# Two attention layers on one core: x in sixteen equal parts almost to the end of the pair tensor, and TensorE's order at the end of the prologue written out with the group norm's sums amid it

## The chip, the cores and the metric

The kernel runs on one core of a Trainium2 chip. The metric is device time in microseconds (us), the median of several runs of the whole kernel. The engines are named as the profile names them: PE (TensorE's matrix multiplications; its weight loads are listed as PEld), DVE (VectorE), ACT (ScalarE), POOL (GpSimd) and SP (SyncE, which here only issues transfers). Each engine works through its own instructions in order and waits where an operand or a buffer isn't ready.

## The reference

The input x has the shape (1, 128, 256, 256): 128 rows of 256 tokens with 256 channels. Two layers are applied, each as x plus an attention over the group norm of x:

```python
def _gn(v, G=32, eps=1e-5):          # over rows, tokens and the channels of a group
    g = v.reshape(B_, H_, W_, G, C_ // G)
    m = jnp.mean(g, axis=(1, 2, 4), keepdims=True)
    s = jnp.var(g, axis=(1, 2, 4), keepdims=True)
    return ((g - m) / jnp.sqrt(s + eps)).reshape(v.shape)

# layer 0: 8 heads of 32 channels, gated, with a bias from the pair tensor
bias = jnp.einsum('nijz,zh->nhij', pair_repr, bias_proj)[:, None]
sim = jax.nn.softmax(einsum(q, k) * scale, axis=-1) + bias
attend = jnp.einsum('nshqk,nskhc->nsqhc', sim, v) * gate

# layer 1: 4 heads of 64 channels, each query sees the keys within 16 positions
x = x + _L0_conv_ref(_gn(x), ...)
x = x + _L1_conv_ref(_gn(x), ..., 16)
```

The group norm needs the mean and the variance of each of 32 groups over the whole of x (32 MiB) before the first row of layer 0 can be normalised. The pair tensor (256 x 256 x 128, 32 MiB as well) is reduced to a bias per head, query and key, which stays on the chip for the whole of layer 0.

## The kernel before

The kernel has three stages: a **prologue** (to about 195 us of the span), **layer 0** and **layer 1**, which handle the 128 rows one after the other. Only the prologue is touched.

The prologue reads pair and x, each once. Its loop (line 479) runs over NM = 32 pieces of the pair tensor, 1 MiB each:

- `load_pair(m)` (422) issues the load of piece m on SP's queue into a ring of five buffers (`pr`).
- `turn_pair(m)` (430): sixteen PE transposes into four PSUM banks (`pz`, line 436), each bank copied out by ACT (`prt`, 438).
- `weigh_pair(m - 1)` (441): four matmuls with the bias weights (`pb`, 445, sixteen records in the profile), copied out by ACT (`bs`, 449).
- `place_bias(m - 2)` (452): four transposes (`pbt`, 461), copied out by ACT (`bq`, 462). After every eighth piece eight more transposes (`pbq`, 470) and two copies (471) write a part of `bias_sb`.

Beside the pieces the loop loads x in NX parts (`x_load`, 320; ring of three `xs` buffers of 2 MiB), also on SP's queue, and DVE takes their sums: `x_stats` (327) issues 32 `bn_stats` for a part, one for each group. Before the change PARTS (317) is fifteen parts of 2 MiB and two of 1 MiB, NX = 17. With AHEAD = 27 the last part is issued at m = 26, behind the load of pair piece 26. At part n the statistics of part n - 2 are issued; at the last part, those of the last two.

The group norm's sums are taken in two steps. `group_most` (209) joins the sums of all parts but the last LATE = 3 (`joined`, 184: seven DVE instructions on 896 elements). After the loop `group_columns` (221) joins this with the last three parts (the `_all` tiles, 224 elements), averages over the partitions with a PE product (`ps_m`, 228), adds the spread between partitions on DVE (230 to 232), brings means and variances into columns with four more PE products (`ps_c`, 245), and takes the root on ACT (254, with a table load in front) and the reciprocal on DVE (`rstd`, 256). Then `weigh_pair(31)`, `place_bias(30)` and `place_bias(31)` follow.

The first two rows of x in the layout of layer 0 come by `load(0)` and `load(1)` (348), four transfers each (`xg`); in before `load(0)` is issued right behind the last part of x, and `load(1)` by the first `normal` of layer 0. Layer 0 begins with `normal(0)` and `normal(1)` (686: DVE transposes `xt` at 523 and the normalisation `xn` at 699), `sum_rows(0)` (705: POOL, `ts`, 552 to 555) and `stretch` (818), whose first products are the PE instructions `pq` of line 577.

What sets the order: in the prologue a scheduler orders each engine's instructions by its own estimate of their times, and the program's order is what it starts from. In layers 0 and 1 the order on PE, ACT and DVE is written out (`tc.manual_schedule`). PSUM has five banks in one ring for all products called `proj` or `sim` in the prologue. The prologue's buffers are given back at its end, and tiles of layer 0 take their place.

Of the kernel before, what the change touches and what calls it, by code (L numbers as in the profile page):

```python
# [39 lines left out]
def conv_preact_kernel(  # L40
# [35 lines left out]
    def proj_bank(name):  # L76
        return bank("proj", name)
# [76 lines left out]
    class Quarters:  # L154
# [9 lines left out]
        def sum(self):  # L164
            s1, s2, s3, s4, n11 = (self.sums[:, n, :] for n in range(len(NS)))
            w00, w10, w01, w11 = (self.quarter(kt, m) for m in range(2) for kt in range(2))
            nc.gpsimd.tensor_tensor(s1, w01, w11, ALU.add)
            nc.gpsimd.tensor_tensor(s2, s1, w00, ALU.subtract)
            nc.gpsimd.tensor_tensor(s3, w00, w01, ALU.subtract)
            nc.gpsimd.tensor_tensor(s4, w10, s2, ALU.subtract)  # L170
            nc.gpsimd.tensor_scalar(n11, w11, -1.0, None, op0=ALU.mult)
# [14 lines left out]
    def joined(pool, mean, squares, sizes, name):  # L186

        n, total = len(sizes), sum(sizes)
        share = pool.tile([P, n], F32, name=f"share_{name}")
        for m, size in enumerate(sizes):  # L190
            nc.gpsimd.memset(share[:, m : m + 1], size / total)
        share = share.unsqueeze(1).to_broadcast([P, G, n])
        dev = pool.tile([P, G, n], F32, name=f"dev_{name}")
        nc.vector.tensor_tensor(dev, mean, share, ALU.mult)
        means = pool.tile([P, G], F32, name=f"means_{name}")
        nc.vector.tensor_reduce(means, dev, axis=AX.X, op=ALU.add)
        nc.vector.tensor_tensor(dev, mean, means.unsqueeze(2).to_broadcast([P, G, n]), ALU.subtract)
        nc.vector.tensor_tensor(dev, dev, dev, ALU.mult)
        nc.vector.tensor_tensor(dev, dev, share, ALU.mult)
        nc.vector.scalar_tensor_tensor(dev, squares, 1.0 / total, dev, op0=ALU.mult, op1=ALU.add)  # L200
        inner = pool.tile([P, G], F32, name=f"inner_{name}")
        nc.vector.tensor_reduce(inner, dev, axis=AX.X, op=ALU.add)
        return means, inner
# [14 lines left out]
        nc.vector.tensor_scalar(last[:, :, 0, 1], inner, sum(halves[0:n]), None, op0=ALU.mult)  # L218
        return last

    def group_columns(pool, last, stats, sizes, which):

        tri, halves = group_shares(stats, sizes)
        n = len(halves) - 2 * LATE
        nc.vector.tensor_copy(last[:, :, 1:, :], tri[:, :, n:, 1:3])
        means, v = joined(pool, last[:, :, :, 0], last[:, :, :, 1], [sum(halves[0:n])] + halves[n:], "all")
        ps_m = proj_bank(f"ps_m{which}")
        nc.tensor.matmul(ps_m[:, 0, 0:G], lhsT=avg, rhs=means, start=True, stop=True)
        d = pool.tile([P, G], F32, name=f"d{which}")
        nc.vector.tensor_tensor(d, means, ps_m[:, 0, 0:G], ALU.subtract)  # L230
        nc.vector.tensor_tensor(d, d, d, ALU.mult)
        nc.vector.tensor_tensor(v, v, d, ALU.add)

        wide = pool.tile([P, 2, 2, A, B // CG, CG], F32, name=f"wide{which}")
        for k, what in enumerate((means, v)):
            by_half = what.rearrange("p (a h u) -> p h a u", a=A, h=2)
            for half in range(2):
                nc.vector.tensor_copy(
                    wide[:, k, half], by_half[:, half].unsqueeze(3).to_broadcast([P, A, B // CG, CG])
                )  # L240
        flat = wide.rearrange("p k h a u c -> p k (h a u c)")
        ps_c = proj_bank(f"ps_c{which}")
        for k in range(2):
            for half in range(2):
                nc.tensor.matmul(
                    ps_c[:, 0, 2 * k + half : 2 * k + half + 1],
                    lhsT=flat[:, k, half * P : (half + 1) * P],
                    rhs=avg[:, 0:1],
                    start=True, stop=True,
                )  # L250
        mean = const.tile([P, 2], F32, name=f"mean{which}")
        nc.vector.tensor_copy(mean, ps_c[:, 0, 0:2])
        std = pool.tile([P, 2], F32, name=f"std{which}")
        nc.scalar.activation(std, ps_c[:, 0, 2:4], AF.Sqrt, bias=eps)
        rstd = const.tile([P, 2], F32, name=f"rstd{which}")
        nc.vector.reciprocal(rstd, std)
        return mean, rstd

    class Most:

# [53 lines left out]
    NT = S * R // P  # L314
    TCH = min(16, NT)

    PARTS = [TCH] * (NT // TCH - 1) + [TCH // 2, TCH // 2]
    NX = len(PARTS)

    def x_load(pool, src, n, name):  # L320
# [27 lines left out]
    def load(g):  # L348
        if g < len(GROUPS) and g not in xgs:
            n, s0 = GROUPS[g], sum(GROUPS[:g])  # L350
            xg = big.tile([P, XG * (R // B), C // A], F32, tag="xg", name=f"xg{g}")
            for a in range(A):
                nc.sync.dma_start(out=xg[strip(a), 0 : n * (R // B)], in_=in_strips(x[0], s0, n, a))
            xgs[g] = xg


    with ExitStack() as early:
        pr_pool = early.enter_context(tc.tile_pool(name="pr", bufs=5))
        xs_pool = early.enter_context(tc.tile_pool(name="xs", bufs=3))
        st_pool = early.enter_context(tc.tile_pool(name="st", bufs=1))  # L360
# [61 lines left out]
        def load_pair(n):  # L422

            qt, jc = divmod(n, R // JC)
            pr = pr_pool.tile([P, JC, Z], F32, tag="pr", name=f"pr{n}")
            nc.sync.dma_start(out=pr, in_=pair[0, qt * P : (qt + 1) * P, jc * JC : (jc + 1) * JC, :])
            prs[n] = pr
# [13 lines left out]
        def weigh_pair(m):  # L441

            pb = ps_av.tile([P, 512], F32, tag=("z", "bv")[m % 2], name=f"pb{m}")
            for g, prt in enumerate(prts.pop(m)):
                nc.tensor.matmul(
                    pb[B * g : B * (g + 1), :], lhsT=bias_w_sb, rhs=prt, start=True, stop=True
                )
            bs = prt_pool.tile([P, 4, P], F32, tag="bs", name=f"bs{m}", bufs=2)
            nc.scalar.copy(bs.rearrange("p i j -> p (i j)"), pb)
            pbs[m] = bs  # L450

        def place_bias(m):

            qt, key = divmod(16 * m, R)
            kt, key = divmod(key, P)
            if key == 0:
                by_query[0] = prt_pool.tile([P, H0, P], F32, tag="bq", name=f"bq{m}", bufs=1)
            bq, bs = by_query[0], pbs.pop(m)
            pt = ps_av.tile([P, 4, 4, B], F32, tag="av", name=f"pbt{m}")
            for i in range(4):  # L460
                nc.tensor.transpose(pt[:, i].rearrange("p g h -> p (g h)"), bs[:, i, :], ident)
            nc.scalar.copy(
                bq[:, :, key : key + 16].rearrange("p h (g i) -> p h g i", i=4),
                pt[:, :, :, 0:H0].rearrange("p i g h -> p h g i"),
            )
            if key == P - 16:
                for h4 in range(0, H0, 4):
                    pq = sim_bank(f"pbq{m}_{h4}").rearrange("p a b -> p (a b)")
                    for h in range(4):
                        nc.tensor.transpose(pq[:, h * P : (h + 1) * P], bq[:, h4 + h, :], ident)  # L470
                    nc.scalar.copy(
                        bias_sb[:, kt, h4 : h4 + 4, qt * P : (qt + 1) * P], pq.rearrange("p (h q) -> p h q", q=P)
                    )
# [1 line left out]
        NM = NPR * (JC // 16)  # L475
        sizes = [k * CG for k in PARTS]

        xss, AHEAD = {}, NM - NM // 6
        for m in range(NM):
            if m % (JC // 16) == 0:  # L480
                load_pair(m // (JC // 16))
            for n in range(m * NX // AHEAD, min((m + 1) * NX // AHEAD, NX)):
                if n == NX - LATE + 2:
                    last = group_most(st_pool, stats, sizes)
                if n >= 2:
                    x_stats(stats, xss[n - 2], n - 2)
                xss[n] = x_load(xs_pool, x[0], n, "0_")
                if n == NX - 1:
                    load(0)
                    for late in (NX - 2, NX - 1):  # L490
                        x_stats(stats, xss[late], late)
            turn_pair(m)
            if m >= 1:
                weigh_pair(m - 1)
            if m >= 2:
                place_bias(m - 2)
            if m == NM // 4:
                load_weights()
                for weights in quarters.values():
                    weights.sum()  # L500
            if m == NM * 3 // 4:
                turn_weights()
        mean0, rstd0 = group_columns(st_pool, last, stats, sizes, 0)
        weigh_pair(NM - 1)
        place_bias(NM - 2)
        place_bias(NM - 1)


    def normalized(pool, xt, mean, rstd, name):
# [846 lines left out]
```

## Time and profile before

| | us |
|---|---|
| median of three runs (lowest, highest) | 3221.67 (3220.45, 3223.09) |
| the profiled execution's own time | 3221.78 |
| its span | 3220.1 |
| PE busy, share of the span | 3135.4 (97%) |
| DVE busy | 2657.6 (83%) |
| last part of x issued, and its statistics done | 150.0 and 172.9 |
| last pair piece issued | 168.3 |
| `rstd` of layer 0 done | 191.9 |
| first product of layer 0 that needs `ts` | 195.6 |

The profile is one execution. Times in it count from the start of the span; "idle before" is the time in which an engine stood still in front of an instruction, with what ended the wait. The table of windows gives each engine's busy time in a stretch, the granted clock of PE (1.00 is full) and the rate of all transfers.

### The profile page before, as it was taken

Reading aid. Unit: us, or ns where it says so; the run is one execution under the profiler, and the core shown is the slowest. Engines: PE = TensorE matmul, PEld = TensorE weight load, DVE = VectorE, ACT = ScalarE, POOL = GpSimd, SP = SyncE. Lnnn points to the kernel's source line nnn. Section 1 sums busy time; section 2 is a strip of 40 time slices with the busy share of each in tenths; the row PEclk is TensorE's granted clock in tenths of the full one; section 3 lists DMA queues with packets and bytes.
Section 4 is the critical chain, followed back from the end, with each engine's and each line's share of the span. In section 5 each row is a group of like instructions: output and inputs, shape, how many; then the busy total and the mean of one; then the engine's idle time right before and its main releaser. Section 6 shows DMA issues by size and latency. Waiting matters only on the chain.

```text
span 3220.1 us, 86853 instructions
## 1 busy us (share of the span) xinstructions
PE 3135.4 (97%) x36965; PEld 2456.0 (76%) x36965; DVE 2657.6 (83%) x3539; ACT 2015.2 (63%) x4316; POOL 1693.7 (53%) x1662
## 2 busy tenths in 40 slices
PE   6799999999999999999999999999999999999997
PEld 4467777777777777777777777678888888888886
DVE  4759999999999999999999999847677777777776
ACT  4566666666666666666666666465666666666664
POOL 3034444444444444444444444287777777777775
PEclk9999999999999999999999999999999999999999
DMA  9931111111111111111111111012222222222222
GB/s 379 421 99 54 48 40 41 34 36 39 40 35 37 38 41 34 38 37 41 34 39 36 41 34 33 22 28 55 67 55 66 67 65 56 67 67 58 64 67 48
DMA packets 346332, 209.38 MB, mean 65 GB/s; under 512 B 273609, under 2 KB 339153, under 8 KB 339665
## 3 DMA queue, kind: packets, MB, share of 16 engines
q1 hardware_dynamic: 345040, 201.37, 21.8%
q8 instruction: 293, 4.80, 0.6%
q0 software_dynamic: 752, 2.36, 0.2%
q14 instruction: 103, 0.84, 0.1%
q10 hardware_dynamic: 144, 0.00, 0.0%
HBM read 136.59 MB, written 67.11 MB: 63 GB/s over the span
## 4 chain that ended last, share of the span: by engine, by line
PE 92%; DMA 4%; DVE 3%; issue 0%; POOL 0%; ACT 0%; SPq 0%; DVEq 0%; ACTq 0%; POOLq 0%
PE sim L717 8%; PE p1v L962 7%; PE 1po L648 7%; PE po L648 7%; PE av L749 7%; PE bv L749 7%; PE pv L581 6%; PE pq L577 6%; PE pk L577 5%; PE p1q L577 5%; PE pg L577 5%; PE p1k L577 5%; PE zs L763 4%; DMA xs<-in_x_dram 4%; PE 1sim L983 3%; PE 1avz L1015 2%
## 5 line engine op out<-in xcount | busy, mean ns | idle before, releaser
L730 ACT ACTIVATE ex<-sim 128x512 f32<-128x512 f32 x1024 | 547.6, 605 | 429.8 <-PE sim L717 429.8
L1043 DVE RECIPROCAL 1rz<-1z 128x512 f32<-128x512 f32 x128 | 427.9, 3343 | 314.8 <-ACT 1z L1037 314.8
L739 DVE TENSOR_TENSOR both<-ex 128x512 f32<-128x512 f32 x512 | 483.8, 983 | 75.4 <-ACT ex L730 75.4
L779 DVE RECIPROCAL d<-d 128x512 f32<-128x512 f32 x128 | 429.1, 3353 | 4.4
L604 POOL TENSOR_TENSOR v<-v,twovg 128x256 f32<-128x256 f32 x64 | 75.5, 1180 | 548.1 <-ACT twovg L622 548.1
L717 PE MATMUL sim<-q,k 32*128 32x256 f32 x4096 | 295.7, 401 | 1.1 <-ACT ex L730 1.1
L648 PE MATMUL po<-at,out_sb 128*128 128x256 f32 x1024 | 285.0, 382 | 4.3 <-DVE at L797 4.3
L648 PE MATMUL 1po<-1at,w_out_t 128*128 128x256 f32 x1024 | 270.2, 388 | 1.1 <-issue 1.0
L717 PEld LDWEIGHTS sim<-q,k 32*128 32x128 f32 x4096 | 186.6, 184 | 102.5 <-issue 94.6
L749 PE MATMUL bv<-bias_sb,v 128*32 128x256 f32 x4096 | 244.5, 379 | 0.7 <-DVE t L794 0.7
L993 POOL TENSOR_TENSOR 1p<-1ex,seen 128x768 f32<-128x768 f32 x128 | 232.5, 1817 | 23.7 <-ACT 1ex L991 23.7
L749 PE MATMUL av<-ex,v 128*32 128x256 f32 x4096 | 244.5, 379 | 0.0
L962 PEld LDWEIGHTS p1v<-w_in_t,1xn 128*64 128x64 f32 x4096 | 222.3, 137 | 21.5 <-issue 21.5
L962 PE MATMUL p1v<-w_in_t,1xn 128*64 128x128 f32 x4096 | 237.7, 274 | 0.3 <-PE warm L886 0.3
L648 PEld LDWEIGHTS 1po<-1at,w_out_t 128*128 128x128 f32 x1024 | 190.3, 191 | 50.2 <-ACT 1z L1037 22.3
L648 PEld LDWEIGHTS po<-at,out_sb 128*128 128x128 f32 x1024 | 185.7, 191 | 25.7 <-issue 4.3
L604 POOL TENSOR_TENSOR q<-q,twoqk 128x256 f32<-128x256 f32 x64 | 48.1, 752 | 297.3 <-ACT twoqk L622 297.3
L749 PEld LDWEIGHTS bv<-bias_sb,v 128*32 128x32 f32 x4096 | 133.2, 110 | 88.7 <-issue 1.1
L749 PEld LDWEIGHTS av<-ex,v 128*32 128x32 f32 x4096 | 133.2, 110 | 87.8 <-issue 0.3
L605 POOL TENSOR_TENSOR 1q<-1q,mid1q 128x512 f32<-128x512 f32 x64 | 81.7, 1277 | 188.6 <-ACT 1q L601 188.6
L699 DVE TENSOR_SCALAR xn<-xt,mean,rstd 128x256 f32<-128x256 f32 x256 | 179.7, 741 | 0.0
L1000 POOL TENSOR_TENSOR 1zp<-1p 128x512 f32<-128x512 f32 x128 | 162.7, 1271 | 10.0
(263 smaller groups left out, 7674.3 us busy)
## 6 DMA issues: line engine op xcount, KB each, us to landing
pr<-in_L_conv_pair_repr_dram SPq DMA_DIRECT2D x32, 1024.0 KB, 23.3
x<-o SPq DMA_DIRECT2D x64, 512.0 KB, 3.0
yg<-x SPq DMA_DIRECT2D x64, 512.0 KB, 4.1
out_dram<-1o SPq DMA_DIRECT2D x256, 128.0 KB, 4.1
xg<-in_x_dram SPq DMA_DIRECT2D x252, 128.0 KB, 3.2
xs<-in_x_dram SPq DMA_DIRECT2D x15, 2048.0 KB, 21.8
xs<-in_x_dram SPq DMA_DIRECT2D x2, 1024.0 KB, 17.6
qkv_sb<-in_L_conv_qkv_proj_dram POOLq DMA_DIRECT2D x4, 192.0 KB, 12.8
```

Of the source, the lines that this page charges most:

```text
L577: nc.tensor.matmul(out, lhsT=weights, rhs=moving, start=first, **flags)
L581: nc.tensor.matmul(out[:, cols], lhsT=moving[:, cols], rhs=weights, start=first and t2 == 0, **flags)
L648: nc.tensor.matmul(ps[:, m, :], lhsT=w[:, kt, m * P : (m + 1) * P], rhs=at[:, kt, :], start=(kt == 0), stop=(kt == 1),)
L699: nc.vector.tensor_scalar(xns[i][:, 2 * r + half, :], xt[:, half, :], mean0[:, half : half + 1], rstd0[:, half : half + 1], op0=ALU.subtra ...
L717: nc.tensor.matmul(sims[j][:, kt, :], lhsT=k[p0 : p0 + D0, 2 * r + half, kt * P : (kt + 1) * P], rhs=q[p0 : p0 + D0, 2 * r + half, :], sta ...
L730: nc.scalar.activation(ex[:, j], sims[j], AF.Exp, scale=1.0 / math.sqrt(D0))
L739: nc.vector.tensor_tensor(both[:, j : j + 2], ex[:, j : j + 2, 0, :], ex[:, j : j + 2, 1, :], ALU.add)
L749: nc.tensor.matmul(to[D0 * j : D0 * (j + 1), half, :], lhsT=v[:, 2 * r + half, c0 : c0 + D0], rhs=weights(4 * half + j, kt), start=(kt == ...
L779: nc.vector.reciprocal(d, d)
L962: nc.tensor.matmul(ps[KB * half : KB * (half + 1), b, :], lhsT=xns[i][:, 2 * r + kt, KB * b : KB * (b + 1)], rhs=w_in_t[:, kt, 2 * C + P * ...
L993: nc.gpsimd.tensor_tensor(p.rearrange("p j (r c) -> p (j r) c", c=WROW)[:, :, 0 : 2 * WSTEP] .rearrange("p r (t c) -> p r t c", c=WSTEP)[: ...
L1043: nc.vector.reciprocal(st[s]["rz"], st[s]["z"])
```

## The change

x comes in sixteen equal parts (`PARTS`), and AHEAD becomes NM - 2 = 30, so that part n is issued at the piece m for which (m + 1) * 16 // 30 first exceeds n: two pieces of pair for a part, in two places one. The last part, number 15, is issued at m = 29; behind it on SP's queue are pair pieces 30 and 31. `group_most` is issued at part 15 too and joins parts 0 to 12.

`load(0)` and `load(1)` move to m = 31, behind the load of pair piece 31.

From m = 29 to the end of the prologue PE's order is the program's. `group_columns` becomes a generator of three pieces: the DVE join of all parts; `ps_m` and the DVE work that follows; `ps_c`, the root and `rstd`. `weigh_pair(31)` comes between the first and the second piece, `place_bias(30)` between the second and the third, and `place_bias(31)` last. On PE this gives, behind the transposes of piece 31: `pb` of 30, `pbt` of 29, `pb` of 31, `ps_m`, `pbt` of 30, `ps_c`, `pbt` of 31, `pbq`.

```diff
@@ -218,12 +218,13 @@
         nc.vector.tensor_scalar(last[:, :, 0, 1], inner, sum(halves[0:n]), None, op0=ALU.mult)
         return last
 
-    def group_columns(pool, last, stats, sizes, which):
+    def group_columns(pool, last, stats, sizes, which, got):
 
         tri, halves = group_shares(stats, sizes)
         n = len(halves) - 2 * LATE
         nc.vector.tensor_copy(last[:, :, 1:, :], tri[:, :, n:, 1:3])
         means, v = joined(pool, last[:, :, :, 0], last[:, :, :, 1], [sum(halves[0:n])] + halves[n:], "all")
+        yield
         ps_m = proj_bank(f"ps_m{which}")
         nc.tensor.matmul(ps_m[:, 0, 0:G], lhsT=avg, rhs=means, start=True, stop=True)
         d = pool.tile([P, G], F32, name=f"d{which}")
@@ -239,6 +240,7 @@
                     wide[:, k, half], by_half[:, half].unsqueeze(3).to_broadcast([P, A, B // CG, CG])
                 )
         flat = wide.rearrange("p k h a u c -> p k (h a u c)")
+        yield
         ps_c = proj_bank(f"ps_c{which}")
         for k in range(2):
             for half in range(2):
@@ -254,7 +256,7 @@
         nc.scalar.activation(std, ps_c[:, 0, 2:4], AF.Sqrt, bias=eps)
         rstd = const.tile([P, 2], F32, name=f"rstd{which}")
         nc.vector.reciprocal(rstd, std)
-        return mean, rstd
+        got += [mean, rstd]
 
     class Most:
 
@@ -314,7 +316,7 @@
     NT = S * R // P
     TCH = min(16, NT)
 
-    PARTS = [TCH] * (NT // TCH - 1) + [TCH // 2, TCH // 2]
+    PARTS = [TCH] * (NT // TCH)
     NX = len(PARTS)
 
     def x_load(pool, src, n, name):
@@ -475,10 +477,16 @@
         NM = NPR * (JC // 16)
         sizes = [k * CG for k in PARTS]
 
-        xss, AHEAD = {}, NM - NM // 6
+        xss, AHEAD = {}, NM - 2
+        tail = early.enter_context(ExitStack())
         for m in range(NM):
+            if m == NM - 3:
+                tail.enter_context(tc.manual_schedule(engines={mybir.EngineType.PE}))
             if m % (JC // 16) == 0:
                 load_pair(m // (JC // 16))
+            if m == NM - 1:
+                load(0)
+                load(1)
             for n in range(m * NX // AHEAD, min((m + 1) * NX // AHEAD, NX)):
                 if n == NX - LATE + 2:
                     last = group_most(st_pool, stats, sizes)
@@ -486,7 +494,6 @@
                     x_stats(stats, xss[n - 2], n - 2)
                 xss[n] = x_load(xs_pool, x[0], n, "0_")
                 if n == NX - 1:
-                    load(0)
                     for late in (NX - 2, NX - 1):
                         x_stats(stats, xss[late], late)
             turn_pair(m)
@@ -500,10 +507,17 @@
                     weights.sum()
             if m == NM * 3 // 4:
                 turn_weights()
-        mean0, rstd0 = group_columns(st_pool, last, stats, sizes, 0)
+        got = []
+        columns = group_columns(st_pool, last, stats, sizes, 0, got)
+        next(columns)
         weigh_pair(NM - 1)
+        next(columns)
         place_bias(NM - 2)
+        for _ in columns:
+            pass
+        mean0, rstd0 = got
         place_bias(NM - 1)
+        tail.close()
 
 
     def normalized(pool, xt, mean, rstd, name):
```

## The prediction

> **What bounds the kernel now.** I first read engine totals and slices on the page, then the prologue by windows, then the single instructions of DVE and PE at its end.
>
> ```profile
> PE 3135.4 (97%) x36965; PEld 2456.0 (76%) x36965; DVE 2657.6 (83%) x3539; ACT 2015.2 (63%) x4316; POOL 1693.7 (53%) x1662
> ...
> GB/s 379 421 99 54 48 40 41 34 36 39 40 35 37 38 41 34 38 37 41 34 39 36 41 34 33 22 28 55 67 55 66 67 65 56 67 67 58 64 67 48
> ```
>
> PE bounds the whole; only the first two slices (80.5 us each) and part of the third run at the memory's rate. Nothing of layers 0 and 1 is edited, so the change can only move the moment at which layer 0 starts: about 195 us of 3220.
>
> ```profile
> 150.00:158.00 8.00, 4.19 (x24) 3.84 (x24) 7.82 (x12) 2.59 (x6) 0.00 (x0) 0.79 1.01 420
> 158.00:168.00 10.00, 9.43 (x75) 7.07 (x73) 10.00 (x60) 7.66 (x23) 0.00 (x0) 1.00 1.06 329
> 168.00:178.00 10.00, 9.63 (x74) 5.78 (x72) 8.05 (x49) 7.51 (x17) 0.00 (x0) 1.00 0.96 348
> 178.00:188.00 10.00, 10.00 (x85) 6.99 (x83) 0.00 (x0) 8.40 (x18) 1.50 (x4) 1.00 0.03 10
> 188.00:196.00 8.00, 5.29 (x37) 3.29 (x36) 4.94 (x15) 3.79 (x8) 4.08 (x11) 1.00 0.24 45
> ```
>
> Columns after the stretch: PE, PEld, DVE, ACT, POOL busy, PE's clock, DMA share, GB/s. Transfers fill the time to about 175. From 158 to 188 PE is full: the loads of x are over after pair piece 26, pieces 27 to 31 then arrive every 2.5 us, and PE needs 3.33 us for one (the `pz` starts 177.66, 181.04, 184.37). So it works off a backlog; the last piece, issued at 168.3, has landed 13.5 us later, at 181.8, and is turned from 184.37. DVE meanwhile is idle.
>
> ```profile
> 172.91 0.36 DVE L225 COPY last<-stats 128x384 f32<-128x384 f32 x1
> ...
> 173.79 0.39 DVE L196 TENSOR_REDUCE means_all<-dev_all 128x32 f32<-128x224 f32 x1
> ...
> 175.94 0.39 DVE L202 TENSOR_REDUCE inner_all<-dev_all 128x32 f32<-128x224 f32 x1
> 188.04 0.19 DVE L230 TENSOR_TENSOR d<-means_all,ps_m 128x32 f32<-128x32 f32 x1 [11.71 <-PE ps_m L228]
> ...
> 191.75 0.17 DVE L256 RECIPROCAL rstd<-std 128x2 f32<-128x2 f32 x1 [1.05 <-ACT std L254]
> ```
>
> The sums of x stand ready at 174.2 and 176.3, and DVE waits 11.7 us for `ps_m`, which is behind the pair's work on PE. The end of PE's part:
>
> ```profile
> 187.69 0.31 PE L228 MATMUL ps_m<-means_all,avg 128*128 128x32 f32 x2
> ...
> 188.35 1.07 PE L445 MATMUL pb<-prt,bias_w_sb 128*32 128x512 f32 x8
> ...
> 195.64 0.70 PE L577 MATMUL pq<-ts,sums_q 128*128 128x256 f32 x2 [1.18 <-POOL ts L552]
> ```
>
> 195.64, the first product that needs `ts`, is my mark for the start of layer 0. Two chains meet there: `rstd`, `xt`, `xn` (third slice about 194.7), and `pb` of piece 31, `pbt`, `pbq`, `bias_sb` (194.69), whose buffers `ts` takes over; the waits name `bias_sb` as releaser.
>
> **The change, part by part.**
>
> *Transfers.* The bytes are the same, and the order on SP's queue differs. Today `load(0)` stands ahead of pieces 27 to 31. Its four issues hold SP from 150.4 to 155.7 (piece 27 goes out at 157.1), and its 256 KB pass slowly: from 160 to 168 the single microseconds moved 251, 241, 246, 251, 360, 380, 365, 393 GB/s, together 0.88 MB below 421 a microsecond, which is 2.1 us; with its own bytes (0.26 MB, 0.6 us) it costs 2.7 us. The Trainium skill, "DMA: Bandwidth & Descriptors", section "Why small descriptors are slow (HBM only)", puts the overhead of 256-byte pieces at 27%, an estimate of 0.26 / 0.421 x 1.27 = 0.8 us; it would leave 1.9 us less of the gain, but the trace has the duration, so I take 2.7. Behind piece 31 both `xg` loads have until about 188 and are hidden; without that cover each costs these 2.7 us again. Their last transfer may go out only when piece 31 has landed (SP waits for older transfers to end); it then lands some 3 us later.
>
> Piece 31 so lands at 181.8 - 2.7 = 179.1. But its landing trails the mean of the engines: pieces 27 to 29 landed at 169.9, 172.5, 174.9, and 30 and 31 at 178.4 and 181.8, 3.4 us apart, while others had begun `load(1)`. Without this growth of 2 us: 177.0. I take T = 178.0. Order at the end: piece 29, x 15 (2 MiB, 5.0 us), 30, 31. With 2.5 to 3.4 us a piece, 30 lands at T - 3.0 = 175.0, x 15 at 172.5, piece 29 at 167.5.
>
> *DVE.* A full part takes 6.28 us (32 `bn_stats`), two halves took 8.4 (67 in 8.76 us): the change saves 2.1. `group_most` is 8.5 us today (150.12 to 159.4 less six `bn_stats` among it) and joins 26 entries in place of 28: 7.9. Part 12 lands 11 MiB ahead of x 15, 27.4 us: 145.1, its statistics end at 151.4. From there DVE has 7.9 + 3 x 6.28 = 26.7 us, to 178.1; by the landing it is 172.5 + 6.28 = 178.8. The later holds: the means stand at 178.8 + 1.3 = 180.1, the variances at 182.2. This is 6 us later than today, hidden as long as PE needs them later still. The buffer of x 15 is that of x 12, free at 151.4, with 21 us of transfers still queued.
>
> *PE.* With x up to piece 29 a piece comes every 4.9 us (1 MiB and 16/30 of 2 MiB at 2.5), against 3.33 of work, so `turn_weights` at piece 24 (some 5 us with its waits) is caught up by 29, done at 170.8, and PE stands still for 4.2 us until 30. The Trainium skill speaks against this: "TensorE: Matmul & The Clock Gate", section "HAM oscillation — how this bites in real kernels", says that gaps over about 3.4 us bring the clock to half. The trace agrees only in part: after 3.13 us idle the transposes of piece 24 took 3.35 us in place of 1.97 (window clock 0.79), after 2.73 us they took 1.97, after 1.16 us 3.65. By the rule piece 30 costs 1.4 more, without it nothing. I take the rule's case, being nearest to the row with 3.13.
>
> So 30: 175.0 + 3.33 + 1.4 = 179.7; 31: 183.1; `pb` of 31, 1.0: `ps_m` at 184.1 (182.7 at full clock; from 182.7 to 185.5 with T from 177 to 179.1). It stood at 187.69. The means, at 180.1, are there. What waits behind `ps_m` in PE's written order, `pbt` of 30 and `ps_c`, waits for nothing else long: `ps_c` needs `wide`, 2.4 us after `ps_m` as today.
>
> *From `ps_m` to the mark.* Today 195.64 - 187.69 = 7.95. In it ACT's table load (1.28 us at 190.16) begins only after the copy of `bs` 31, and DVE waits 1.05 for the root. Now `pb` 31 is ahead of `ps_m`, so copy and table load fit into the 2.85 us before `ps_c` ends: 0.9 less, or nothing if the scheduler leaves the load late. Take 7.5. The other chain: `ps_c` ends at ps_m + 2.85, `pbt` of 31 to `bias_sb` took 191.93 to 194.69 = 2.76, so ps_m + 5.6: ahead of `ts` at + 6.7. POOL's `sums_1q` to `most` (186.5 to 191.0), released by the last `pz`, moves forward with it and stays ahead of `ts`.
>
> *Sum.* Mark at 184.1 + 7.5 = 191.6 instead of 195.64: **4.0 us earlier**. Split: 3.8 from the transfers (181.8 to 178.0), 2.6 from the backlog on PE that goes (184.37 - 181.8), less 1.7 because the transposes of 31 start that long after it lands (1.4 of it the half clock), less 1.0 for `pb` 31 ahead of `ps_m`, and 0.45 from the table load; the parts are rounded. From the profiled execution: 3220.1 - 4.0 = 3216.1, plus the 1.7 outside the span, 3217.8; it lies 0.1 above the median, so **3217.7**. The generator and `tail.close()` issue nothing; their cost is the order above.
>
> **Rivals.**
>
> *The landing trails no more* (C). If every engine ends piece 31 near the mean, which the fall of the rate at 175 puts at 175.2 today, T is 175.2 - 2.7 + 2 = 174.5, `ps_m` at 180.6 and the mark near 188: 7.6 us gained, 3214.1. For it: nothing small lies ahead of piece 31 now. Against: part 14, landing at 152.1 long before any `xg`, trailed by about 4.5 us as well.
>
> *The clock* (B). PE has little work between `ps_m` and the mark, about 3 of 7.5 us, where it had more. A half clock in the first products costs up to 3.6 us: at 211.5 to 218.7 it holds for 7.2 us today (window clock 0.57). Then the gain is 0.4: 3221.3. Against it: 188 to 196 has PE at 5.3 of 8 us and a full clock behind it.
>
> *x comes too late* (D, the other side). `ps_m` now stands ahead of all PE work that is left, so late sums hold TensorE. Place: x 15's 2 MiB, behind x 12's statistics on SP's queue. Gain is nil when the means come at 195.6 - 7.5 = 188.1, 8.0 us later than worked out; from there every microsecond is lost. If DVE puts `group_most` and part 13 ahead of part 12's release (12 us more), 3225.7. Against: today part 16 goes out at 150.04, right as part 13's statistics end, ahead of `group_most`.
>
> *It doesn't take effect* (E): the scheduler already ordered PE well, and the transposes bound either way; 3221.
>
> **How the numbers follow.** 0.2% is 6.4 us, about what a measurement of this kernel can tell from no change. A 0.50 (its own range 3216 to 3219.5), B and E 0.24, C 0.18, D 0.08. The range drops the lower tail of C and most of D: 3213.0 to 3222.0. Faster by over 0.2% is C, 0.18; slower by over 0.2% needs D with 14 us: 0.05; within is the rest, 0.77.
>
> **What would show it.** Right: last `xs` landing near 172 and piece 31 near 178; `pz` of 30 behind a wait for `pr`; `ps_m` near 184 with DVE's wait ahead of `d` down from 11.7 to about 2; the mark near 191.6; layer 0 unchanged in length. Wrong: `ps_m` waiting for `means_all` (D), a clock under 0.8 between 192 and 212 (B), piece 31 before 176 (C), or a layer 0 whose rows take another time than today's 14.6 us each.

## The result and the profile after

| | before | changed |
|---|---|---|
| median of 15 runs each, us (lowest, highest) | 3221.21 (3219.84, 3223.69) | 3214.99 (3211.97, 3217.99) |
| ratio to before, 95% interval | | 0.998, 0.9972 to 0.9988 |
| span of the profiled execution | 3220.1 | 3214.2 |
| last transfer of x issued | 150.0 | 153.0 |
| pair piece 31 landed | 181.8 | 179.0 |
| means of all parts ready (`means_all`) | 174.2 | 181.4 |
| `ps_m` | 187.69 | 183.51 |
| mark: first product that needs `ts` | 195.64 | 190.50 |
| first `zs` of layer 0 | 224.6 | 219.7 |
| first product of layer 1 (`p1v`) | 2092.5 | 2087.3 |

The change gains 6.2 us of 3221; the interval allows 3.9 to 9.0. A second measurement of the changed kernel (below) gave 0.9984, 0.9977 to 0.9991, which is 5.1 us. In the two traces the mark is 5.14 us earlier, and 4.9 and 5.2 of this are left at the first `zs` and at the start of layer 1. So the gain is made in the prologue and kept. The spans differ by 5.9 us; the last 0.7 arises in layer 1, which the change doesn't touch and which took from 1125.3 to 1128.8 us in the profiles of all the kernels here but the one with six products more.

The windows of the changed kernel's profile, in the columns of the table before (PE, PEld, DVE, ACT, POOL busy, PE's clock, DMA share, GB/s):

```profile
150.00:158.00 8.00, 7.64 (x58) 4.79 (x56) 7.80 (x21) 5.95 (x15) 0.00 (x0) 1.00 1.01 425
158.00:168.00 10.00, 4.10 (x34) 2.82 (x32) 9.93 (x38) 4.14 (x9) 0.00 (x0) 0.92 1.00 422
168.00:178.00 10.00, 8.21 (x51) 5.42 (x49) 10.00 (x53) 4.93 (x10) 0.00 (x0) 0.74 0.88 281
178.00:188.00 10.00, 8.83 (x71) 5.89 (x64) 8.49 (x31) 6.63 (x14) 4.91 (x12) 0.95 0.05 11
188.00:196.00 8.00, 7.30 (x31) 5.42 (x29) 4.88 (x13) 4.20 (x9) 4.32 (x6) 0.85 0.82 131
```

The roles have changed. From 158 to 168 PE is busy for 4.1 of 10 us where it was full, and DVE now works without a break from 150 to 186. The transfers keep 422 GB/s between 158 and 168, where the early `load(0)` had brought them down to 329. DVE's instructions in order of time:

```profile
146.66 0.16 DVE L417 TENSOR_TENSOR bo_v<-pbias_v,bo 128x2 f32<-128x2 f32 x1 [6.00 <-PE pbias_v L413]
146.74 6.27 DVE L332 BATCH_NORM_STATS2 stats<-xs 128x6 f32<-128x128 f32 x32
...
161.67 18.43 DVE L332 BATCH_NORM_STATS2 stats<-xs 128x6 f32<-128x128 f32 x95
...
184.34 0.18 DVE L231 TENSOR_TENSOR d<-means_all,ps_m 128x32 f32<-128x32 f32 x1
```

The wait of 11.7 us in front of `d` is gone: `d` follows its own engine's work, so in this execution DVE and not PE came last there. The first line shows something that the prediction hadn't seen. `bo_v`, the sum of two bias columns, stands in DVE's queue ahead of part 12's statistics and waits 6.0 us for PE; part 12 had landed at 144.2. PE at the end of the prologue:

```profile
167.52 3.65 PE L438 MATMUL pz<-ident,pr 128*128 128x128 f32 x16 [5.47 <-DMA pr<-in_L_conv_pair_repr_dram]
...
175.54 1.94 PE L438 MATMUL pz<-ident,pr 128*128 128x128 f32 x16 [1.79 <-DMA pr<-in_L_conv_pair_repr_dram]
...
179.04 1.97 PE L438 MATMUL pz<-ident,pr 128*128 128x128 f32 x16
...
182.52 1.06 PE L447 MATMUL pb<-prt,bias_w_sb 128*32 128x512 f32 x8
183.51 0.41 PE L229 MATMUL ps_m<-means_all,avg 128*128 128x32 f32 x2
...
187.01 1.97 PE L472 MATMUL pbq<-ident,bq 128*128 128x128 f32 x8 [0.36 <-ACT bq L464]
...
190.50 0.70 PE L591 MATMUL pq<-ts,sums_q 128*128 128x256 f32 x2 [0.67 <-POOL ts L566]
```

Pieces 29, 30 and 31 (the three `pz`) are turned as they land; the backlog is gone. The eight `pbq` took 1.97 us instead of 1.09, at half clock.

### The profile page after: what moved, and what is told of

It is laid out like the page before. It is cut to its first block, busy times and chain, and to the rows that moved or that the text cites. A ratio compares the mean times of both kernels' runs of the same rounds, so it can differ in the third digit from the quotient of the medians.

```text
span 3214.2 us, 86812 instructions
## 1 busy us (share of the span) xinstructions
PE 3131.4 (97%) x36965; PEld 2454.8 (76%) x36965; DVE 2656.1 (83%) x3507; ACT 2014.7 (63%) x4316; POOL 1691.9 (53%) x1660
## 4 chain that ended last, share of the span: by engine, by line
PE 92%; DMA 4%; DVE 3%; POOL 0%; issue 0%; ACT 0%; SPq 0%; DVEq 0%; ACTq 0%; POOLq 0%
PE sim L731 8%; PE p1v L976 7%; PE 1po L662 7%; PE po L662 7%; PE av L763 7%; PE bv L763 7%; PE pv L595 6%; PE pq L591 6%; PE p1q L591 5%; PE pk L591 5%; PE pg L591 5%; PE p1k L591 5%; PE zs L777 4%; PE 1sim L997 3%; PE 1avz L1029 2%; DMA pr<-in_L_conv_pair_repr_dram 2%
## 5 line engine op out<-in xcount | busy, mean ns | idle before, releaser
L619 POOL TENSOR_TENSOR 1q<-1q,mid1q 128x512 f32<-128x512 f32 x64 | 81.6, 1275 | 189.3 <-ACT 1q L615 189.3
```

## The experiments

The reading that was to be tested: the gain comes from the moment at which x and the pair pieces land, and from the backlog on PE that the even spread removes. Its rivals: the written order earns it; the early `load(0)` alone costs it; or one engine sets the end whatever else moves. All marks, each of one profiled execution, beside the times of 9 to 21 runs. The marks are good to about 2 us: among the six executions with the changed kernel's loads and written order (the changed kernel twice, `bo_v` on ACT, both kernels with `ps_m` sooner, six products more) piece 29 landed from 165.8 to 167.8.

| kernel | `ps_m` | mark | first `zs` | median us | ratio to before, interval |
|---|---|---|---|---|---|
| moved loads alone | 182.23 | 191.03 | 220.0 | 3216.41 | 0.9984, 0.9978 to 0.9991 |
| order alone | 187.82 | 194.50 | 222.1 | 3220.09 | 0.9995, 0.9987 to 1.0003 |
| `load(0)` moved alone | 189.75 | 197.70 | 223.5 | 3222.52 | 1.0007, 0.9998 to 1.0015 |
| the same, with the order | 188.93 | 195.60 | 223.1 | 3221.20 | 1.0000, 0.9991 to 1.0008 |
| changed, `load(0)` early | 187.13 | 193.74 | 224.4 | 3217.85 | 0.9991, 0.9982 to 0.9999 |
| changed, x last | 189.70 | 198.13 | 226.7 | 3223.35 | 1.0006, 0.9998 to 1.0015 |
| changed, x sooner | 183.78 | 190.45 | 218.1 | 3215.65 | 0.9981, 0.9973 to 0.9990 |
| changed, once more | 183.35 | 190.05 | 215.9 | 3216.24 | 0.9984, 0.9977 to 0.9991 |
| changed, `bo_v` on ACT | 184.78 | 191.39 | 218.9 | 3214.54 | 0.9979, 0.9971 to 0.9987 |
| the same, `ps_m` ahead of `pb` 31 | 181.87 | 189.50 | 217.0 | 3213.17 | 0.9975, 0.9965 to 0.9985 |
| the same again | 184.25 | 191.88 | 219.4 | 3213.97 | 0.9977, 0.9970 to 0.9984 |
| changed, six products more | 185.66 | 192.27 | 218.4 | 3220.48 | 0.9996, 0.9987 to 1.0004 |

### The moved loads alone

The even parts, AHEAD = 30 and both `xg` loads behind piece 31 stay; PE's order is the scheduler's again, and all of `group_columns` comes ahead of `weigh_pair(31)`.

```diff
-            if m == NM - 3:
-                tail.enter_context(tc.manual_schedule(engines={mybir.EngineType.PE}))
...
-        columns = group_columns(st_pool, last, stats, sizes, 0, got)
-        next(columns)
-        weigh_pair(NM - 1)
-        next(columns)
-        place_bias(NM - 2)
-        for _ in columns:
+        for _ in group_columns(st_pool, last, stats, sizes, 0, got):
             pass
         mean0, rstd0 = got
+        weigh_pair(NM - 1)
+        place_bias(NM - 2)
         place_bias(NM - 1)
-        tail.close()
```

> The moved loads of x and xg as in the changed kernel, but TensorE's order left to the scheduler, the group norm's sums all ahead of the last pb. Theory (the gain comes from when transfers land and from the backlog that goes): mark (first pq that needs ts) at 190 to 191.5, within 1 us of the changed kernel's 190.5; total 3215 to 3216. Rival (the written order earns it): mark at 193 or later, total 3218 or more.

PE's last instructions in that kernel:

```profile
182.23 0.41 PE L229 MATMUL ps_m<-means_all,avg 128*128 128x32 f32 x2
...
191.03 0.70 PE L584 MATMUL pq<-ts,sums_q 128*128 128x256 f32 x2 [1.11 <-POOL ts L559]
```

The mark is 0.5 us behind the changed kernel's, and the total is 4.4 us below before. The moved loads earn most of the gain (4.6 of 5.14 us at the mark). The scheduler even put `ps_m` 1.3 us sooner; this brings little, since DVE isn't through with the variances (184.7). The equal parts, the later AHEAD and the later `xg` loads come together here; the first two were not run apart.

### The order alone

The written order and the split sums, with x in 15 + 2 parts, AHEAD = 27 and `load(0)` early.

```diff
-    PARTS = [TCH] * (NT // TCH)
+    PARTS = [TCH] * (NT // TCH - 1) + [TCH // 2, TCH // 2]
...
-        xss, AHEAD = {}, NM - 2
+        xss, AHEAD = {}, NM - NM // 6
...
-            if m == NM - 1:
-                load(0)
-                load(1)
...
                 if n == NX - 1:
+                    load(0)
```

> The written order of TensorE and the split sums alone, with x in 15 + 2 parts and load(0) as before the change. Theory: TensorE still has its backlog, piece 31 is turned at 184.4, pb of 31 now stands ahead of ps_m at 188.7, and 7.0 us later the mark is at 195.7: no gain, total 3221 (3220 to 3222). Rival (the written order earns it): mark at 192 or earlier, total 3217 or less.

```profile
183.40 1.91 PE L438 MATMUL pz<-ident,pr 128*128 128x128 f32 x16
...
186.82 1.07 PE L447 MATMUL pb<-prt,bias_w_sb 128*32 128x512 f32 x8
187.82 0.41 PE L229 MATMUL ps_m<-means_all,avg 128*128 128x32 f32 x2
...
194.50 1.22 PE L589 MATMUL pq<-ts,sums_q 128*128 128x256 f32 x2 [0.96 <-POOL ts L564]
```

The backlog stays: piece 31 is turned at 183.4, one us sooner than before, and `ps_m` is where it was, with `pb` of 31 already done. From `ps_m` to the mark it is 6.7 us instead of 7.95. So in this profile the order gains 1.1 us at the mark where I had expected none, and 0.8 in the median, which the interval can't tell from nothing.

### `load(0)` alone, without and with the order

Before the change, with only this edit; then the same edit in the kernel of the order alone.

```diff
+            if m == NM - 1:
+                load(0)
+                load(1)
...
                 if n == NX - 1:
-                    load(0)
```

> Before the change, with load(0) and load(1) alone moved behind pair piece 31. Theory: pieces 27 to 31 land 2 to 3 us sooner, but TensorE is full from 158 on, so the mark moves by 0 to 1 us only (194.6 to 195.6), total 3220 to 3221.5. Rival (the 2.7 us that load(0) costs the transfers are worth 2.7 us by themselves): mark at 193, total 3218.5.

> As the kernel with load(0) and load(1) alone moved behind piece 31 (mark 197.7), plus the written order of TensorE, x still in 15 + 2 parts. Theory (that kernel lost 2 us because the scheduler, on other estimates, put copies' waits between the pieces: 4.0 us a piece instead of 3.33): 3.33 us a piece again, mark at 194.5 as with the order alone, total 3220. Rival (moving load(0) delays something else): mark at 196 or later, total 3222.

PE without the written order:

```profile
183.74 1.91 PE L436 MATMUL pz<-ident,pr 128*128 128x128 f32 x16
...
187.68 1.91 PE L436 MATMUL pz<-ident,pr 128*128 128x128 f32 x16
```

and with it:

```profile
181.18 1.91 PE L438 MATMUL pz<-ident,pr 128*128 128x128 f32 x16
...
184.51 1.91 PE L438 MATMUL pz<-ident,pr 128*128 128x128 f32 x16
```

Both expectations for the first kernel fell: its mark is 2.1 us later than before, not sooner. A piece takes 3.94 us (183.74 to 187.68): the scheduler mixed the pieces otherwise, and the `pb` of one took 1.8 to 2.0 us in place of 1.07. With the order written out it is 3.33 again. But the second kernel doesn't reach the 194.5 of the order alone either. Its first piece behind `turn_weights` starts no sooner, and a piece ahead of the written part is again in the slower mix (`pb` of 2.0 us at 174.1). Clear is the main point: piece 31 landed at 178.1 and 178.8 instead of 181.8, PE didn't wait for a piece from 160 on, and nothing was gained (1.0007, 0.9998 to 1.0015, and 1.0000, 0.9991 to 1.0008). With a backlog on PE sooner transfers were worth nothing here, so the price of an early `load(0)` can't be read from the transfers' windows alone.

### The changed kernel with `load(0)` early

```diff
             if m == NM - 1:
-                load(0)
                 load(1)
...
                 if n == NX - 1:
+                    load(0)
```

> The changed kernel with load(0) put back right behind the last part of x, ahead of pair pieces 30 and 31. Theory: these land 2.7 us later (178.2 and 181.7 instead of 175.5 and 179.0) and TensorE follows: ps_m at 186, mark at 193, total 3217.5. Rival (load(0) is hidden there too): mark at 190.5, total 3215.

```profile
177.72 3.57 PE L438 MATMUL pz<-ident,pr 128*128 128x128 f32 x16 [5.32 <-DMA pr<-in_L_conv_pair_repr_dram]
...
193.74 0.70 PE L591 MATMUL pq<-ts,sums_q 128*128 128x256 f32 x2 [1.48 <-POOL ts L566]
```

With no backlog the same load costs 3.2 us at the mark. Piece 30 landed at 177.6 (2.2 later) and piece 31 at 180.1 (1.1 later); the rest is the half clock, 3.57 us for the transposes of piece 30 after a wait of 5.3. In the medians the cost is 2.9 us against the first measurement of the changed kernel and 1.6 against the second.

### x last, and x sooner

AHEAD = 32 puts part 15 behind piece 31, AHEAD = 28 ahead of piece 28.

```diff
-        xss, AHEAD = {}, NM - 2
+        xss, AHEAD = {}, NM
```

```diff
-        xss, AHEAD = {}, NM - 2
+        xss, AHEAD = {}, NM - 4
```

> The changed kernel with AHEAD = 32: the last part of x goes out behind pair piece 31. Theory (the sums of x set the end once they come later than TensorE's part): x 15 lands at 179 instead of 172.4, its statistics end at 185.3, inner_all at 189, and 6.2 us behind d the mark is at 195: 4.5 later than in the changed kernel, total 3219.5. Rival (TensorE's pair work sets the end whatever x does): pieces 30 and 31 land 5 us sooner, mark at 190 or earlier, total 3215 or less.

> The changed kernel with AHEAD = 28: the last part of x goes out at piece 27, so four pieces of pair follow it. Theory (a backlog of pair pieces on TensorE then sets the end): pieces 28 to 31 land every 2.5 us and take 3.33 each, ps_m at 185.8 instead of 183.5, mark at 192.4, total 3217. Rival (DVE's statistics set the end in the changed kernel, so sooner is better): mark at 189 or earlier, total 3214 or less.

x last, on DVE and then on PE:

```profile
182.05 6.28 DVE L332 BATCH_NORM_STATS2 stats<-xs 128x6 f32<-128x128 f32 x32 [8.82 <-DMA xs<-in_x_dram]
```

```profile
189.70 0.64 PE L229 MATMUL ps_m<-means_all,avg 128*128 128x32 f32 x2 [10.44 <-DVE means_all L196]
```

`ps_m` waits 10.4 us for the means, as the rival of the other side described it, and the kernel is slower than before at the mark by 2.5 us. The part landed at 182.0, 3 us later than I had expected. I had overlooked that the edit leaves it behind the `xg` loads on SP's queue: their last transfer went out at 173.4, as piece 31 landed, and part 15 only at 173.8. And PE, idle for so long, ran the whole of the next stretch at half clock: 0.53 between 182 and 200. Both together made the mark 3 us later than the theory had it; how much a part directly behind piece 31 would lose wasn't run.

x sooner, on DVE:

```profile
184.22 0.19 DVE L231 TENSOR_TENSOR d<-means_all,ps_m 128x32 f32<-128x32 f32 x1 [7.76 <-PE ps_m L229]
```

Here DVE waits 7.8 us for PE, and yet the mark, 190.45, is the changed kernel's. The backlog is 2 us smaller than I had expected (`ps_m` at 183.78, not 185.8): part 15 landed at 166.7, and pieces 28 to 31 at 169.2, 171.7, 174.7 and 178.3. Neither of the two expectations was met. Between 28 and 30 the choice of AHEAD makes no difference that these runs can tell; at 32, with the `xg` loads in front of the part, it loses the whole gain.

### `bo_v` off DVE, and `ps_m` sooner

The first kernel computes `bo_v` on ACT; the second also puts `ps_m` ahead of `pb` of piece 31. The changed kernel and the second ran again on the same chip as the first.

```diff
-            nc.vector.tensor_tensor(bo_v, pv[:, 0:2], bo, ALU.add)
+            for m in range(2):
+                nc.scalar.activation(bo_v[:, m : m + 1], pv[:, m : m + 1], AF.Identity, bias=bo[:, m : m + 1])
```

```diff
         next(columns)
+        next(columns)
         weigh_pair(NM - 1)
-        next(columns)
         place_bias(NM - 2)
```

> The changed kernel with bo_v computed by ACT alone, the written order kept (pb of 31 ahead of ps_m). Theory (DVE set the end by half a microsecond): means at 180, mark 0.5 sooner than in the changed kernel, total 0.5 less. Rival (the sooner ps_m is what made the kernel with both 1.8 faster): no difference from the changed kernel.

> The changed kernel with bo_v computed by ACT, so that it does not hold part 12's statistics on DVE, and with ps_m ahead of pb of 31. Theory (in the changed kernel DVE's statistics end 1.5 us late because bo_v waits 6.0 us ahead of them, and DVE then sets the end by half a microsecond): means at 180.0 instead of 181.4, mark at 189.3, total 3214. Rival (TensorE alone sets the end): mark at 190.5, total 3215.

> The changed kernel once more, on the same chip as the two kernels with bo_v on ACT. Theory: a mark at 190.5 to 192.3 (the later one where the transposes of piece 30 fall into a half clock), total 3215 to 3216.

> The kernel with bo_v on ACT and ps_m ahead of pb of 31, beside the changed kernel on the same chip. Theory: mark about 1 us sooner than in the changed kernel, total 3213 to 3214 where the changed kernel has 3215.

DVE and PE of the kernel with `bo_v` alone on ACT:

```profile
144.22 6.28 DVE L332 BATCH_NORM_STATS2 stats<-xs 128x6 f32<-128x128 f32 x32 [3.58 <-DMA xs<-in_x_dram]
...
185.22 0.19 DVE L231 TENSOR_TENSOR d<-means_all,ps_m 128x32 f32<-128x32 f32 x1 [3.16 <-PE ps_m L229]
```

```profile
175.45 3.48 PE L439 MATMUL pz<-ident,pr 128*128 128x128 f32 x16 [2.38 <-DMA pr<-in_L_conv_pair_repr_dram]
```

Part 12's statistics now start as it lands, and the means stand at 179.9, 1.5 us sooner, as expected. But `d` waits for `ps_m` all the same, because this execution turned piece 30 at half clock. The changed kernel's second profile shows the same case:

```profile
173.95 2.90 PE L438 MATMUL pz<-ident,pr 128*128 128x128 f32 x16 [1.88 <-DMA pr<-in_L_conv_pair_repr_dram]
...
183.79 0.19 DVE L231 TENSOR_TENSOR d<-means_all,ps_m 128x32 f32<-128x32 f32 x1 [1.60 <-PE ps_m L229]
```

So which of the two sets the end, PE or DVE, changes from execution to execution with the clock of one piece. Of the four marks that I had expected, only that of the first kernel with both was met (189.3; 189.50). The kernel with `bo_v` alone had 191.39, which is later than the changed kernel and not 0.5 sooner. The changed kernel's second mark was 190.05 in spite of the half clock, as its transfers landed 1.5 us sooner (piece 31 at 177.5). The second profile of the kernel with both is 1.8 behind that. In the medians, on one chip, the changed kernel took 3216.24, with `bo_v` on ACT 3214.54, with both 3213.97; the kernel with both had 3213.17 the first time. Both measurements of the last are below both of the changed kernel, by 1 to 3 us, but the intervals overlap: it had the lowest median here, and its lead isn't settled. Its two marks (189.50, 191.88) lie on both sides of the changed kernel's (190.50, 190.05).

### Six products more

```diff
                         attend(s - 1)
+                        if s == 0:
+                            hot = ps_av.tile([P, 2, R], F32, tag="av", name="hot")
+                            for _ in range(6):
+                                nc.tensor.matmul(hot[:, 0, :], lhsT=ident, rhs=out_sb[:, 0, :], start=True, stop=True)
                         last_exp = scores(s, 1)
```

> The changed kernel with six products more (they write a bank that nothing reads) between the first and the second half of row 0's scores, where TensorE waits 1.1 us for the exponentials and runs at half clock for 7 us right after. Theory (the clock falls because TensorE does little in that stretch): no half clock between 204 and 215, the first zs 2 to 3 us sooner after the mark (26 to 27 us instead of 29.2), total 3212. Rival (the clock falls for another reason, or not for these 1.1 us): the first zs 29 us or more after the mark, total 3215 to 3215.5.

The window from 204 to 215, in the columns above, first of the changed kernel, then of this one, then of the changed kernel once more:

```profile
204.00:215.00 11.00, 9.90 (x47) 7.21 (x40) 4.59 (x8) 8.21 (x14) 6.00 (x6) 0.69 0.00 0
```

```profile
204.00:215.00 11.00, 10.98 (x73) 8.61 (x72) 4.44 (x8) 9.73 (x17) 7.05 (x8) 1.00 0.00 0
```

```profile
204.00:215.00 11.00, 9.87 (x56) 6.76 (x52) 5.24 (x8) 9.86 (x19) 7.16 (x9) 1.00 0.00 0
```

The half clock is gone with the products, and the first `zs` comes 26.1 us after the mark, as the theory had it. But in the second profile of the changed kernel the half clock is gone without them, so this doesn't show that they did it. That is inconclusive. And the total rose by 4.2 to 5.5 us where 3 less were expected. The profile places it: between 2200 and 2400, in layer 1, PE was busy for 193.7 us instead of 198.5, with one stop of 0.6 to 1.2 us a round in front of `1avz` that the profile puts down to nothing. Why 12 more products and their 12 weight loads in row 0 of layer 0 go with this wasn't found.

## Why the prediction held, step by step

The predicted time was 3217.7 with a range from 3213.0 to 3222.0; measured were 3214.99 and, again, 3216.24. The direction and the mechanism held; 4.0 us were forecast, and the gain is 6.2 (3.9 to 9.0), or 5.1 by the traces and by the second measurement. By its median it stayed just under my boundary of 6.4 us for faster by over 0.2%; its interval takes that boundary in.

- **What bounds.** The reading that PE's backlog, and not the transfers, set the start of layer 0 was right: the transfers sooner by themselves gained nothing, and the even spread with the later `xg` loads, without the order, gained 4.4 us.
- **Transfers.** The landing times came out close: piece 29 at 167.4 (forecast 167.5), part 15 at 172.3 (172.5), piece 30 at 175.4 (175.0), piece 31 at 179.0 (178.0). The term of 3.8 us thus was 2.8 here and 4.3 in the changed kernel's second profile, where piece 31 landed at 177.5. For `load(0)` I took 2.7 from the rates and put aside the estimate of 0.8 from the Trainium skill ("DMA: Bandwidth & Descriptors", section "Why small descriptors are slow (HBM only)"). The page's 27% are 3 of 11 cycles, so the factor should have been 11/8 and not 1.27; the estimate is then 0.85 us. Put back, `load(0)` delayed piece 30 by 2.2 and piece 31 by 1.1 us, between the two.
- **DVE.** The means came at 181.4, not 180.1, and the variances at 184.4, not 182.2. That DVE's sums would be hidden behind PE therefore failed in this execution, where DVE was the last by half a microsecond; in the five others with these loads and this order DVE did wait for `ps_m`, 0.9 to 3.2 us, in three of them with `bo_v` on ACT. The step that failed is that I placed `turn_weights` on PE alone: its last instruction, `bo_v`, is DVE's, and waited in front of part 12's statistics. On ACT it gives the means at 179.9. The rest of the delay, 3.02 us instead of 2.15 from means to variances, falls together with POOL's `sums_1q` and `sums_1k` (181.2 to 186.1). No run was made for this, but the kept traces agree: the same work took 3.02 and 3.07 us in the two in which POOL ran through all of it, 2.35 where POOL began 1.2 us into it, and 2.15 in the ten others that can be compared, POOL beginning in the last 0.7 us of it or later. Some of POOL's instructions became longer as well (0.60 us in place of 0.45).
- **PE.** I had one stand of 4.2 us ahead of piece 30. There are two, 5.47 ahead of 29 (part 14 lies between 28 and 29) and 1.79 ahead of 30. (A piece comes every 5.2 us and not every 4.9: 2.07 MiB at 2.5.) The half clock of piece 29 is hidden. Piece 30 kept the full clock in the first profile and in one other, and had 2.90, 3.40, 3.48 and 3.65 us in four with the same loads. The rule of 3.4 us that I took from the Trainium skill ("TensorE: Matmul & The Clock Gate", section "HAM oscillation — how this bites in real kernels") would have charged nothing for the waits of 1.7 to 2.8 us that piece 30 really had; that my 1.4 us fit four of the six is luck. In the first profile the term of 1.7 is 0: piece 31 is turned as it lands. In the changed kernel's second profile it is 1.4.
- **From `ps_m` to the mark** it was 6.99, against 7.5 taken and 7.05 as the bound. The table load did move out of the way: it starts at 184.71, and DVE waits 0.33 us for the root instead of 1.05.
- **The sum by its terms,** as measured in the first profile: 2.8 + 2.6 - 0.0 - 1.15 + 0.96 = 5.2, against 3.8 + 2.6 - 1.7 - 1.0 + 0.45. Two terms were sized wrongly for that execution and partly cancelled: the transfers 1.0 too large, the clock 1.7 too dear. The second profile gives 4.3 + 2.6 - 1.4 - 1.1 + 1.25 = 5.6. The first and the third term thus change from execution to execution by 1.5 us, and that the forecast came within 1 to 2 us of the gain is in part luck.
- **The rivals.** The late sums (D) came out near their price: with the means at 189.65, 9.6 behind my figure and so 1.6 behind the point from which every microsecond is lost, the kernel lost 2.3 us against the kernel before, measured beside it (3221.04), and 2.5 at the mark. The half clock made `ps_m` to the mark 8.4 us instead of 7.5. The clock (B) was there, in `pbq` at 187 and again from 207 to 214, and cost no more than before the change, which had it from 212 to 219 (29.2 us from the mark to the first `zs`, against 29.0). That the landing trails no more (C) didn't come: piece 31 landed at 179.0.

## What to carry to other kernels

When two streams share the memory's bandwidth and each feeds another engine, spread them so that the engine with the longer work for each byte doesn't get a long run of its own pieces at the end (five were too many here; between four and two no difference was seen); what counts is which engine is still working when the last byte has landed, and a cheaper transfer is worth nothing to an engine with a backlog. Move the last part of the other stream only so far that its own tail (here statistics of 6.3 us, a join of 3, a few products) ends with the first engine's; two pieces of pair behind it were right, and with none, and the `xg` loads ahead of the part, the gain was gone. And when engines are balanced this closely, list what else stands in their queues: one addition of 0.16 us, waiting for another engine, held the next statistics back by 2.4 us and the means by 1.5.

## What the runs showed of the hardware

The length of a wait alone didn't decide whether PE lost its full clock. In the six executions with the changed kernel's loads and written order the sixteen transposes of piece 30 took 1.94 us after waits of 1.73 and 1.79 us, and 2.90, 3.40, 3.48 and 3.65 us after 1.88, 2.18, 2.38 and 2.81 us. But before the change one piece took 1.97 us after a wait of 2.73, and one 3.65 after 1.16.

The clock record of the traces says more. In each of the fourteen traces the granted clock changes only on a grid of 3.41 us, whose place differs from execution to execution, and a spell of half clock lasts one or more whole steps. From 80 to 180 us of the spans there are 354 steps at full clock. After the 33 in which PE was busy for less than 43% of the step half clock always followed; after the 299 with more than 49% it never did; 22 lie between, with both. In the step whose end decided over piece 30, PE was busy for 48 and 49% in the two executions that kept the full clock and for 36 to 45% in the four that lost it. So it mattered where the grid fell on the wait. This is a count and no experiment; and behind the pair pieces half clock also followed ten steps with 68 to 79%, begun between 183 and 214 us, so busy time alone isn't the whole measure.

Two profiles of one kernel differ by 3.4 us between the mark and the first `zs` (29.2 and 25.8), more than half of what the change gains: the first had half clock from 207.4 to 214.2, the second none there, and half of these 6.8 us is the difference. After the 10.4 us of waiting for the late sums the clock was halved for five steps, from 183.2 to 200.3, with PE busy for half of the time.
